# One list of threads at the end of attention, and three products of the last block on GpSimd instead of VectorE

## The chip, the cores and the metric

The kernel runs on one core of a Trainium2 chip. The metric is the device time of one execution in microseconds (us), a median over several executions. A profiled execution gives a trace beside it. Engines are called by the names of the profile: PE is TensorE, PEld its weight loads, DVE is VectorE, ACT is ScalarE, POOL is GpSimd, SP is SyncE, which issues most DMAs.

## What is computed

One layer of a transformer, in float32, on x of 4 x 1024 tokens with 256 channels. First a causal attention over the 1024 tokens with 16 heads of 16 and a linear bias by distance; then, with "tokens" and "batch" in other roles, a second attention in which each of the 1024 positions attends over the 4 rows of the batch, and a mixture of 8 experts in which each token takes the larger of its two best experts' numbers:

```
x = x + (softmax(q k^T / 4 + bias) v) @ w_proj.T        # q, k, v from layernorm(x)
u = layernorm(x)
q, k, v = split(u @ in_proj_w.T + in_proj_b)            # per token and row of the batch
attn = softmax(q[t] . k[s] / 4 over the 4 rows s)       # scores of 4 x 4 x 16 per position
h = layernorm(u + (attn v) @ out_w.T + out_b)
assign = max(top_2(softmax(h @ router_w.T + router_b)))
oe = gelu(h @ w1[assign].T + b1[assign]) @ w2[assign].T + b2[assign]
out = x + layernorm(h + oe)
```

## The kernel before

All of the time is in one function, fast_layer. (general_layer, behind a flag, is a fallback which isn't run with these inputs.) The order of the instructions on each engine is the order in which the program issues them; the program plans that order by a small model of costs while it is built.

**Attention** (up to about 606 us). The work goes by units of tokens and by rounds: score a round (matmuls into sk, exponential on ScalarE into p), mask with a select on GpSimd (line 1038), weigh it (matmuls of p with v into pv, line 1044), copy the result yt, and store it. Each round has slots into which the program places work for VectorE and TensorE that falls due (E_slot, D_slot, take_E, take_D, lines 2156 to 2326). A finished unit is divided by its sums of exponentials, projected by w_proj and added to x. For most units the sums go through DRAM (load_sums, invert, load_inverse, divide, project; lines 1104 to 1150): the product yc x su, then matmuls op<-wp,yc, then the addition (add_attended, line 1137). The last unit does it on the chip: a matmul adds up the slots (sum<-yt,slot_sum), VectorE takes the reciprocal and multiplies (yn; normalise, line 1172), four matmuls project (op<-wp_slots,yn; project_slots, line 1181), and the result is added to x.

**The fronts.** A front (line 1615) takes the 4 rows of the batch at 128 positions, a block, through the second attention up to the router. It is a generator that yields before each piece of work the letter of the engine that decides it and a cost. Its steps: statistics of the four x (norm_stats), their root on GpSimd (norm_root, line 828), u, transposes (ut), qkv by matmuls, four score products pr of 128 x 1024 each followed by a reduction (sc), the softmax, four weighted products pv of 128 x 1024 each followed by transposes into PSUM (ctp), copies (ct), matmuls with w_out (ao), additions to u, layer norm (rstd_h, by a root on GpSimd), the router, and the placing of tokens in lists by expert. There are 8 blocks, numbered 0 to 7. Fronts run between the rounds of attention; block 6 is under way at attention's end, and block 7, "the last block", follows it. In the last block the score and weighted products go one by one, with tile work between (lines 1703 to 1770).

**Expert tiles.** Each tile takes up to 128 tokens of one expert: GpSimd gathers their rows by an indirect DMA (given<-rows, line 1889), TensorE transposes (mtp), ScalarE scales (mt), TensorE multiplies by w1 (hid), ScalarE does the gelu (ge), TensorE multiplies by w2 (oe), VectorE takes statistics (stats_v), GpSimd or VectorE the root, VectorE makes the result in place in the gathered tile (given), and GpSimd clears a spare word (line 2005) and stores by an indirect DMA (out_dram<-given, line 2006). Groups of up to two tiles take their root on GpSimd (line 829); larger groups take it by a Newton step on VectorE (norm_root_v, line 833). 34 tiles are done: 18 from a first table, which needs the first six blocks alone, and 16 from a second table, which needs the last block's placing (the matmuls who, at 681 us). The gathered tiles live in N_GIVEN = 20 buffers, used in turn; LANDING = 2 keeps some of them free. The first four tiles have their experts' weights loaded by themselves; all later tiles use the whole of w1 and w2 in SBUF (load_layer, line 2395, three DMAs on SP for each).

**The end of attention and the tail.** Behind the last rounds (line 2376 on) the program issues one after another what is left of attention: what is due on VectorE, normalise(2) and normalise(3), project_slots, the last unit but one's division and projection, the last store of y and load of sums. Only then does it build `threads`, with block 7's front first, the unfinished fronts (block 6) and the preparation of the second table behind it, and plan them against the tiles: of the threads it takes the one that can begin first by the model, and a tile step where TensorE would be idle before it (lines 2440 to 2500). At least HELD_BACK = 5 tiles are kept for the time in which the second table is made.

Of the kernel before, what the change touches and what calls it, by code (L numbers as in the profile page):

```python
# [29 lines left out]
F32 = mybir.dt.float32  # L30
# [7 lines left out]
P = 128  # L38
# [26 lines left out]
TURNED = 2  # L65
EARLY = 0
N_OWN = 4
N_GIVEN, LANDING = 20, 2
N_W1 = 3
HELD_BACK = 5  # L70

TILE = (("PE", 2.6), ("DVE", 1.7), ("ACT", 1.9), ("POOL", 2.3))
TILE_HALF, LAG, COPIED, FIRST_BY, W1_THERE, LOAD_W2 = 1.3, 0.2, 1.0, 0.1, 14.0, 2.0
KQ_BUFS = 2
D_SLOT = 10.0
SWITCH, COLUMN, EXP_AT_ALL, EXP, READ = 0.2, 1 / 600, 0.17, 1 / 1200, 0.7
AHEAD, EARLY_BY, ROOT, OF_D = 1.0, 0.2, 1.4, 0.35
SUMS_BY, INVERTED_BY, Y_BY, DIVIDED_BY, PROJECTED_BY = 7.0, 14.0, 16.5, 26.0, 28.0
NEVER, HURRIED = 1e6, {SUMS_BY: 2.0, INVERTED_BY: 5.5, Y_BY: 7.5}
# [529 lines left out]
def fast_layer(ctx: ExitStack, tc: tile.TileContext, odd, x, wq, wk, wv, wp, w_in, w_out, w_r,  # L609
# [60 lines left out]
    def bank(name):  # L670
        if tail_banks:
            return tail_banks[0].tile([P, QC], F32, tag="m", name=name)
        if half_of:
            return half_of.pop()
        pair = pair_of_banks(name)
        halves[pair.tensor.name] = [], []
        half_of.append(pair[:, 1])
        return pair[:, 0]
# [51 lines left out]
    def wide(a):  # L730
        return a.unsqueeze(1).to_broadcast([P, B] + list(a.shape)[1:])
# [90 lines left out]
    def norm_stats(src, n, name, tag=""):  # L822
        tiles = norm_tiles(name, tag)
        for i in range(n):
            norm_one(tiles, i, src(i))
        return norm_end(tiles, n)
# [310 lines left out]
    def add_attended(u, pm):  # L1137
        n, i, size = units[u]
        at = xs[batches[n]][:, i:i + size].rearrange("p n c -> p (n c)")
        nc.vector.tensor_tensor(at, at, pm[:, :size * C], ALU.add)  # L1140

    def project(u):
        yc = held.pop(("y", u))
        pm = bank(f"op_{u}")
        for i in range(units[u][2]):
            for cc in range(CC):
                nc.tensor.matmul(
                    pm[:, i * C:(i + 1) * C], yc[:, cc, i * P:(i + 1) * P], wp_sb[:, cc],
                    start=cc == 0, stop=cc == CC - 1,
                )  # L1150
        add_attended(u, pm)


    slot_sum = const("slot_sum", [P, P])
# [14 lines left out]
                )  # L1169
            held["wp"].append(w)  # L1170

    def normalise(g):
        if g % 2 == 0:
            held["yn", g // 2] = ends.tile([P, 2, W], F32, tag="su", name=f"yn_{g}", bufs=2)
        yt, yn = (held[k, g // 2][:, g % 2, :P] for k in ("yt", "yn"))
        pm = bank(f"sum_{g}")[:, :P]
        nc.tensor.matmul(pm, slot_sum, yt, start=True, stop=True)
        nc.vector.reciprocal(yn, pm)
        nc.vector.tensor_tensor(yn, yn, yt, ALU.mult)

    def project_slots():
        pm = bank(f"op_{last_unit}")
        for g in range(G):
            nc.tensor.matmul(
                pm[:, :C], held["yn", g // 2][:, g % 2, :P], held["wp"][g // 2][:, g % 2],
                start=g == 0, stop=g == G - 1,
            )
        add_attended(last_unit, pm)


    def numbered(name, shape, pattern, up=0, base=0, dtype=F32, into=keep):
# [423 lines left out]
    def front(i, fact, more, last):  # L1615
# [1 line left out]
        xi = [xs[i // PC, t] for t in range(B)]  # L1617
        at_x = lambda t: xi[t][:, i % PC]
        rows_of = part.rows_of.rearrange("(k t p) c -> k p t c", t=B, p=P)[i]
        yield "E", 2.5  # L1620
        mv, rstd = norm_stats(at_x, B, f"u_{i}")
        yield "R", 1.2
        norm_root(rstd, B)
        yield ("A" if last else "P"), 1.9
# [71 lines left out]
            routed()  # L1696

        sc = fact.tile([P, B, B, H], F32, tag="sc", name=f"sc_{i}")
        for t in range(B):
            yield "E", 2.4, 0.9 if last else 0.0  # L1700
            if last:
                projected_qkv(t, QC, 3 * C + E)
            pr = fact.tile([P, B, C], F32, tag="pr", name=f"pr_{i}_{t}")
            nc.vector.tensor_tensor(pr, wide(qk[:, t, 0:C]), qk[:, :, C:], ALU.mult)
            nc.vector.tensor_reduce(
                sc[:, t], pr.rearrange("p s (h d) -> p s h d", d=D), AX.X, ALU.add
            )
# [16 lines left out]
        nc.vector.reciprocal(tot, tot)  # L1724
        nc.vector.tensor_tensor(sc, sc, each_s(tot), ALU.mult)

        def weighted(t):
            pr = fact.tile(
                [P, B, C], F32, tag="ctx" if last and t % 2 else "pr", name=f"pv_{i}_{t}"
            )  # L1730
            nc.vector.tensor_tensor(
                pr.rearrange("p s (h d) -> p s h d", d=D),
                vr[:, :, 0:C].rearrange("p s (h d) -> p s h d", d=D),
                sc[:, t].unsqueeze(3).to_broadcast([P, B, H, D]),
                ALU.mult,
            )
            return pr

        if last:

            ct = fact.tile(
                [P, CC, QC], F32, tag="turned", name=f"ct_{i}", bufs=TURNED if more else 2
            )

            def turned_sum(t, pr):
                pt = bank(f"ctp_{i}_{t}")[:, :C].rearrange("p (c q) -> p c q", q=P)

                for cc in range(CC):
                    for k in range(B):
                        nc.tensor.matmul(  # L1750
                            pt[:, cc], pr[:, k, cc * P:(cc + 1) * P], ident,
                            is_transpose=True, start=k == 0, stop=k == B - 1,
                        )
                nc.scalar.copy(ct[:, :, t * P:(t + 1) * P], pt)

            pr = None
            for t in range(B):
                yield "E", 1.3, 1.0 if t else 0.0
                if t:
                    turned_sum(t - 1, pr)  # L1760
                pr = weighted(t)
            yield "D", 1.0
            turned_sum(B - 1, pr)
            for t in range(B):
                for_later(t)
            store(("x", i), store_later)
        else:
            ctx_ = fact.tile([P, B, C], F32, tag="ctx", name=f"ctx_{i}")
            for t in range(B):
                yield "E", 2.3  # L1770
                pr = weighted(t)
                nc.vector.tensor_tensor(pr[:, 0:2], pr[:, 0:2], pr[:, 2:4], ALU.add)
                nc.vector.tensor_tensor(ctx_[:, t], pr[:, 0], pr[:, 1], ALU.add)
# [356 lines left out]
    def busy(on, cost, ready=0.0):  # L2130
        time[on] = max(time[on], ready) + cost
        return time[on]
# [119 lines left out]
    def projected(u):  # L2252
        n, i, size = units[u]
        c = batches[n][0]
        project(u)
        for k in range(PC * c + i, PC * c + i + size):
            n_projected[k] += 1
            if n_projected[k] == B and k < NT - 1:
                queue.append(front(k, fact, 1, False))
# [41 lines left out]
    def E_slot(k, some=True):  # L2301
        for cost, what in of_E.pop(k, []) + pop_due(due_E, time["PE"]):
            what()
            busy("DVE", cost)
        issue_stores(age=1)
        for it in stores:
            it[1] += 1
        load_next()
        if tables and fetching:
            experts.fetch()  # L2310
        take_E(some)
# [43 lines left out]
    for p in range(len(rounds) // 2):  # L2355
        then = p < len(rounds) // 2 - 1
        score_next(2 * p)
        E_slot(2 * p)
        D_slot(p, then)
        fill()  # L2360
        take_E(then)
        score_next(2 * p + 1)
        if len(waiting) > 2:
            weigh_next(waiting[:2])
            del waiting[:2]
        fill()
        E_slot(2 * p + 1, then)
# [6 lines left out]


    assert not of_E and not of_D, (sorted(of_E), sorted(of_D))

    take_E()
    for g in range(2, G):
        normalise(g)  # L2380
        busy("DVE", 1.3)
    project_slots()
    for _, what in pop_due(due_E, 2 * NEVER) + pop_due(due_D, 2 * NEVER):
        what()
    issue_stores(age=0)
    load_sums(last_unit)
    for it in running:
        it.ready = 0.0
    tail = ctx.enter_context(pool("tail", 1))
# [5 lines left out]
    def load_layer(sb, src):  # L2395
        for lo, hi in ((1, 3), (3, 5), (5, E)):
            nc.sync.dma_start(sb[:, lo - 1:hi - 1], src[:, lo:hi])
# [27 lines left out]
            n_bad, n_good, -1.0, float(B * NT * H), ALU.mult, ALU.add  # L2425
        )

    of_late = [(LOAD_W2, lambda: load_layer(w2_sb, w2))]

    late["at_place"] = ends.tile([P, 2 * B, P], BF16, tag="su", name="at_places", bufs=2)  # L2430

# [5 lines left out]

    threads = [Running(front(NT - 1, fact, 1, True))] + running + [Running(prepare_rest())]  # L2440
    free = {"PE": 0.0, "DVE": 0.0, "ACT": 0.0, "POOL": 0.0}
    threads[0].ready = 0.0
    engine_of = {"E": "DVE", "P": "DVE", "A": "ACT", "N": "ACT", "R": "POOL", "D": "PE", "d": "PE"}

    def begin(it):
        if it.kind == "DQ" and ("qkv",) in held or it.kind[1:] == "C" and part.placed < NT - 1:
            return 1e9
        return max(it.ready, free[engine_of[it.kind[0]]])

# [13 lines left out]
            threads.remove(it)  # L2463

    def tile_begin():
        return max(free["PE"], W1_THERE if experts.n_fetched > 2 * N_OWN else 0.0)

    def tile_step(finish=True):
        at = tile_begin()
# [135 lines left out]
```

## Time and profile before

| | us |
|---|---|
| median of 5 runs (lowest to highest) | 762.64 (762.23 to 764.65) |
| the profiled execution | 764.41 |
| its span in the trace | 762.7 |
| final weighing of attention begins | 603.67 |
| first score product of the last block | 634.40 |
| last matmul of its ao | 662.33 |
| TensorE's last matmul | 742.73 |
| last store of a tile ends | 751.83 |

| engine | busy us | share of the span |
|---|---|---|
| PE | 686.6 | 90% |
| PEld | 516.7 | 68% |
| DVE | 519.5 | 68% |
| ACT | 426.2 | 56% |
| POOL | 235.5 | 31% |

A line of the timeline has the start in us, the duration, engine, line, operation, output<-inputs with partitions x elements, and in brackets the idle time of the engine before it and what ended it. A group's line has its count, the busy time and the mean ns of one, and the idle time ahead with its releasers. Most instructions are recorded by one helper and stand at L590; they are told apart by the names of their tiles. A matmul of float32 is two rows in the trace. The table of windows gives each engine's busy time within a stretch, the granted TensorE clock as a share of full speed (PEclk), and the DMA engines' busy share.

### The profile page before, as it was taken

To read this page: it belongs to the slowest core of one execution; us is meant where nothing else is said; L and a number is where in the kernel's file an instruction comes from. 1 tells how busy PE (TensorE), PEld (TensorE's weight loads), DVE (VectorE), ACT (ScalarE), POOL (GpSimd) and SP (SyncE) were. 2 spreads that over 40 slices of the span, in tenths; PEclk is the share of its full clock that TensorE was granted. 3 is DMA by queue.
4 is the path that set the end of the run, shared out by engine and by line. 5 is a ranking of instruction groups with operands and counts; after the bars stand their busy time and mean duration, and the time that the engine had idled before them with its cause. 6 is when DMAs were issued, how large, how long until landed. Compare 5 with 4: busy or idle time off the path is not lost. (4 is left out here: it accounts for less than half of the span.)

```text
span 762.7 us, 21784 instructions
## 1 busy us (share of the span) xinstructions
PE 686.6 (90%) x8877; PEld 516.7 (68%) x8877; DVE 519.5 (68%) x1312; ACT 426.2 (56%) x647; POOL 235.5 (31%) x335
## 2 busy tenths in 40 slices
PE   3889899999999999999898999999999787989990
PEld 2667677675665766667567887678868655879980
DVE  4546437566996674889854163979769969699972
ACT  1446456563656574565556765658657435467750
POOL 4453213130332220023311130213212421268883
PEclk9999999999999999999899999999999989899995
DMA  7535453432363332323326543434343392154431
GB/s 217 154 114 174 153 181 118 136 118 82 91 190 99 102 107 93 109 88 104 121 77 211 179 150 93 165 113 146 113 137 102 89 310 96 33 169 145 147 103 35
DMA packets 70871, 98.46 MB, mean 129 GB/s; under 512 B 15408, under 2 KB 54635, under 8 KB 70252
## 3 DMA queue, kind: packets, MB, share of 16 engines
q1 hardware_dynamic: 58528, 67.82, 28.6%
q10 hardware_dynamic: 7884, 16.05, 6.6%
q0 software_dynamic: 4352, 13.11, 5.6%
q8 instruction: 73, 1.20, 0.6%
q14 instruction: 34, 0.28, 0.1%
HBM read 60.50 MB, written 34.59 MB: 125 GB/s over the span
## 5 line engine op out<-in xcount | busy, mean ns | idle before, releaser
L590 ACT ACTIVATE p<-sk 128x1024 f32<-128x1024 f32 (+1 forms) x320 | 288.0, 940 | 147.7 <-PE sk L590 120.8
L1038 POOL TENSOR_SCALAR_AFFINE_SELECT p<-p 128x512 f32<-128x512 f32 (+1 forms) x160 | 107.9, 679 | 403.1 <-ACT p L590 400.5
L590 PE MATMUL sk<-slots 32*128 32x128 f32 (+1 forms) x3456 | 178.1, 327 | 11.1 <-DVE kq L590 4.3
L590 PEld LDWEIGHTS sk<-slots 32*128 32x128 f32 x3456 | 135.0, 187 | 53.6 <-issue 24.2
L590 PE MATMUL pv<-p,v 128*32 128x128 f32 (+1 forms) x3456 | 145.3, 315 | 7.8 <-ACT p L590 4.0
L590 PEld LDWEIGHTS pv<-p,v 128*32 128x32 f32 x3456 | 96.0, 111 | 46.6 <-ACT p L590 8.0
L590 PE MATMUL qkvp<-w_in,ut 128*128 128x264 f32 (+1 forms) x240 | 83.5, 486 | 0.2 <-ACT ut L590 0.2
L590 PEld LDWEIGHTS qkvp<-w_in,ut 128*128 128x128 f32 x240 | 42.5, 190 | 28.8 <-issue 24.3
L590 PE MATMUL qkp<-xt,wqk 128*128 128x256 f32 x224 | 56.3, 396 | 0.2 <-ACT p L590 0.2
L590 DVE COPY kq<-qkp 128x512 f32<-128x512 f32 x28 | 19.1, 685 | 48.6 <-PE qkp L590 48.6
L590 PEld LDWEIGHTS qkp<-xt,wqk 128*128 128x128 f32 x224 | 41.4, 194 | 10.9 <-issue 3.3
L590 PE MATMUL hid<-mt,w 128*128 128x128 f32 x272 | 40.9, 287 | 2.6 <-ACT ge L590 1.7
L590 DVE TENSOR_TENSOR pv<-vr,sc 128x1024 f32<-128x1024 f32 x32 | 39.6, 1239 | 3.8 <-PE ctp L590 3.5
L590 ACT COPY qkv<-qkvp 128x512 f32<-128x512 f32 x28 | 16.4, 586 | 44.9 <-PE qkvp L590 44.7
L590 DVE COPY vr<-qkvp 128x264 f32<-128x264 f32 x28 | 12.1, 431 | 42.4 <-PE qkvp L590 42.4
L590 DVE TENSOR_REDUCE sc<-pr 128x64 f32<-128x1024 f32 x32 | 39.0, 1220 | 1.1
L590 DVE TENSOR_TENSOR pr<-qkv 128x1024 f32<-128x1024 f32 x32 | 39.2, 1224 | 0.5 <-ACT qkv L590 0.2
L1889 POOL DMA_INDIRECT given<-rows,rows x34 | 36.3, 1066 | 10.0 <-issue 7.9
L590 PEld LDWEIGHTS hid<-mt,w 128*128 128x128 f32 x272 | 36.6, 195 | 3.8 <-ACT ge L590 2.2
L2006 POOL DMA_INDIRECT out_dram<-given,out_rows x34 | 34.4, 1011 | 7.6 <-issue 3.6
L590 PE MATMUL oe<-w,ge 128*128 (+1 forms) x136 | 35.9, 387 | 0.0
L590 PE MATMUL vp<-wv,xt 128*128 128x256 f32 x128 | 34.4, 415 | 0.0
(327 smaller groups left out, 980.5 us busy)
## 6 DMA issues: line engine op xcount, KB each, us to landing
slots<-k SPq DMA_DIRECT2D x32, 320.0 KB
k<-kq SPq DMA_DIRECT2D x32, 256.0 KB
v<-v ACTq DMA_DIRECT2D x4, 1152.0 KB
x<-in_x_dram SPq DMA_DIRECT2D x16, 256.0 KB
y<-yt SPq DMA_DIRECT2D x16, 256.0 KB
rows<-x SPq DMA_DIRECT2D x32, 128.0 KB
slots<-k SPq DMA_DIRECT2D x16, 256.0 KB
rows<-u SPq DMA_DIRECT2D x8, 512.0 KB
```

Of the source, the lines that this page charges most:

```text
L590: ins = made(*args, **kwargs)
L1038: nc.gpsimd.affine_select(blocks, blocks, pattern=[[0, 2], [0, size], [1, P]], compare_op=ALU.is_ge, fill=0.0, base=0, channel_multiplier=-1,)
L1889: nc.gpsimd.indirect_dma_start(out=self.hx, out_offset=None, in_=t.rows_of, in_offset=bass.IndirectOffsetOnAxis(ap=t.rows_[:, self.j:self. ...
L2006: ins = nc.gpsimd.indirect_dma_start(out=out.rearrange("t n c -> (t n) c"), out_offset=bass.IndirectOffsetOnAxis(ap=t.table.out_rows[:, t. ...
```

## The change

1. **One list of threads.** What was issued in a row at attention's end becomes two threads, last_slots and last_but_one, ahead of block 7's front in `threads`. project and project_slots return their PSUM tile, and the caller adds it to x. normalise's matmul is split off (sum_slots). In the last pair of rounds E_slot doesn't issue VectorE's due work any more, so this too is planned with the threads. The front takes the statistics of x one by one; in the last block the third and fourth wait until both units have been added ("EX"). The weight loads of w1 and w2 go ahead of the last store of y and the sums on SP (LOAD_SUMS).
2. **Products on GpSimd in the last block.** Of the four score products pr, GpSimd makes the second and the fourth; of the four weighted products pv, the fourth. They share one buffer of 4 KB a partition ("shared", one deep).
3. **Room for it.** N_GIVEN goes from 20 to 18 and LANDING from 2 to 1.
4. The planner's costs: tiles begin at 9.5 (OWN_THERE) and 20 (W1_THERE, before 14) by the model's clock.

```
-N_GIVEN, LANDING = 20, 2
+N_GIVEN, LANDING = 18, 1
...
-        add_attended(u, pm)
+        return pm
...
-        yield "E", 2.5
-        mv, rstd = norm_stats(at_x, B, f"u_{i}")
+        tiles = norm_tiles(f"u_{i}")
+        yield "E", 1.2 if last else 2.5
+        for t in range(B):
+            if last and t == B - 2:
+                yield "EX", 1.4
+            norm_one(tiles, t, at_x(t))
+        mv, rstd = norm_end(tiles, B)
...
+        shared = lambda name: late["work"].tile([P, B, C], F32, tag="shared", name=name, bufs=1)
+        def multiplied(t, engine, pr):
+            engine.tensor_tensor(pr, wide(qk[:, t, 0:C]), qk[:, :, C:], ALU.mult)
+            return pr
         for t in range(B):
-            yield "E", 2.4, 0.9 if last else 0.0
+            if last and t % 2 == 0:
+                by_pool = multiplied(t + 1, nc.gpsimd, shared(f"pr_{i}_{t + 1}"))
+            yield "E", 1.2 if last and t % 2 else 2.4, 0.9 if last else 0.0
...
-            pr = None
-            for t in range(B):
+            pr, by_pool = None, weighted(B - 1, nc.gpsimd)
+            for t in range(B - 1):
                 yield "E", 1.3, 1.0 if t else 0.0
                 if t:
                     turned_sum(t - 1, pr)
                 pr = weighted(t)
-            yield "D", 1.0
-            turned_sum(B - 1, pr)
+            yield "D", 2.0
+            turned_sum(B - 2, pr)
+            turned_sum(B - 1, by_pool)
...
-        E_slot(2 * p)
+        E_slot(2 * p, then)
...
-    take_E()
-    for g in range(2, G):
-        normalise(g)
-        busy("DVE", 1.3)
-    project_slots()
-    for _, what in pop_due(due_E, 2 * NEVER) + pop_due(due_D, 2 * NEVER):
-        what()
-    issue_stores(age=0)
-    load_sums(last_unit)
...
-    of_late = [(LOAD_W2, lambda: load_layer(w2_sb, w2))]
+    of_late = [(LOAD_W2, lambda: load_layer(w2_sb, w2)), (LOAD_SUMS, lambda: load_sums(last_unit))]
...
+    def last_slots():
+        yield "D", 0.5
+        pms = [sum_slots(g) for g in range(2, G)]
+        yield "E", 2.6
+        for g in range(2, G):
+            normalise(g, pms[g - 2])
+        yield "D", 1.8
+        pm = project_slots()
+        yield "E", 0.5
+        add_attended(last_unit, pm)
+        added.append(last_unit)
+
+    def last_but_one():
+        u = last_unit - 1
+        yield "E", 0.5
+        divide(u)
+        yield "D", 0.9
+        pm = project(u)
+        yield "E", 0.5
+        add_attended(u, pm)
+        added.append(u)
```

In the compiled order of the instructions, these move on each engine:
- VectorE: yn_1 and the statistics of x_0 and x_1 stand right after the first weighted product of block 6; yc x su after its second; yn_2, yn_3 and the addition to x_2 after its third; then the fourth, the addition to x_3, ct's copy and the statistics of x_2 and x_3. The statistics and root of the first pair of tiles (stats_v_0) go from between the last block's first two weighted products to behind its router.
- TensorE: op<-wp,yc goes ahead of op<-wp_slots; one tile step (mtp of one tile, hid and oe of earlier ones) goes from ahead of the last block's transposes to behind its ao.
- GpSimd: pr_1 stands ahead of the fifth gather, pr_3 ahead of the sixth, pv_3 ahead of the eighth. In the tail two groups of two tiles fewer take their root on GpSimd.
- SP: the last store of y and the sums stand behind the loads of w1 and w2.

More of the change, by code (lines that the diff above doesn't have):

```diff
@@ L72 @@
 TILE = (("PE", 2.6), ("DVE", 1.7), ("ACT", 1.9), ("POOL", 2.3))
-TILE_HALF, LAG, COPIED, FIRST_BY, W1_THERE, LOAD_W2 = 1.3, 0.2, 1.0, 0.1, 14.0, 2.0
+TILE_HALF, LAG, COPIED, FIRST_BY, OWN_THERE, W1_THERE, LOAD_W2, LOAD_SUMS = (
+    1.3, 0.2, 1.0, 0.1, 9.5, 20.0, 8.0, 10.0,
+)
 KQ_BUFS = 2
@@ L76 @@
 SWITCH, COLUMN, EXP_AT_ALL, EXP, READ = 0.2, 1 / 600, 0.17, 1 / 1200, 0.7
+LAST_SUMS = 3.7
 AHEAD, EARLY_BY, ROOT, OF_D = 1.0, 0.2, 1.4, 0.35
@@ L1170, in load_slotted, with sum_slots, normalise @@
             held["wp"].append(w)
-    def normalise(g):
+    def sum_slots(g):
+        pm = bank(f"sum_{g}")[:, :P]
+        nc.tensor.matmul(pm, slot_sum, held["yt", g // 2][:, g % 2, :P], start=True, stop=True)
+        return pm
+    def normalise(g, pm=None):
         if g % 2 == 0:
@@ L1175, in normalise @@
         yt, yn = (held[k, g // 2][:, g % 2, :P] for k in ("yt", "yn"))
-        pm = bank(f"sum_{g}")[:, :P]
-        nc.tensor.matmul(pm, slot_sum, yt, start=True, stop=True)
+        if pm is None:
+            pm = sum_slots(g)
         nc.vector.reciprocal(yn, pm)
@@ L1187, in project_slots @@
             )
-        add_attended(last_unit, pm)
+        return pm
     def numbered(name, shape, pattern, up=0, base=0, dtype=F32, into=keep):
@@ L1698, in front @@
         sc = fact.tile([P, B, B, H], F32, tag="sc", name=f"sc_{i}")
+        shared = lambda name: late["work"].tile([P, B, C], F32, tag="shared", name=name, bufs=1)
+        def multiplied(t, engine, pr):
+            engine.tensor_tensor(pr, wide(qk[:, t, 0:C]), qk[:, :, C:], ALU.mult)
+            return pr
         for t in range(B):
-            yield "E", 2.4, 0.9 if last else 0.0
+            if last and t % 2 == 0:
+                by_pool = multiplied(t + 1, nc.gpsimd, shared(f"pr_{i}_{t + 1}"))
+            yield "E", 1.2 if last and t % 2 else 2.4, 0.9 if last else 0.0
             if last:
                 projected_qkv(t, QC, 3 * C + E)
-            pr = fact.tile([P, B, C], F32, tag="pr", name=f"pr_{i}_{t}")
-            nc.vector.tensor_tensor(pr, wide(qk[:, t, 0:C]), qk[:, :, C:], ALU.mult)
+            if last and t % 2:
+                pr = by_pool
+            else:
+                pr = multiplied(
+                    t, nc.vector, fact.tile([P, B, C], F32, tag="pr", name=f"pr_{i}_{t}")
+                )
             nc.vector.tensor_reduce(
@@ L1725, in front, with weighted @@
         nc.vector.tensor_tensor(sc, sc, each_s(tot), ALU.mult)
[L1727 to L1731, printed above, removed]
+        def weighted(t, engine=nc.vector):
+            if engine is nc.gpsimd:
+                pr = shared(f"pv_{i}_{t}")
+            else:
+                pr = fact.tile(
+                    [P, B, C], F32, tag="ctx" if last and t % 2 else "pr", name=f"pv_{i}_{t}"
+                )
+            engine.tensor_tensor(
                 pr.rearrange("p s (h d) -> p s h d", d=D),
@@ L2254, in projected @@
         c = batches[n][0]
-        project(u)
+        add_attended(u, project(u))
         for k in range(PC * c + i, PC * c + i + size):
@@ L2436, in prepare_rest @@
         part.prepare_rest(1)
-    threads = [Running(front(NT - 1, fact, 1, True))] + running + [Running(prepare_rest())]
-    free = {"PE": 0.0, "DVE": 0.0, "ACT": 0.0, "POOL": 0.0}
-    threads[0].ready = 0.0
+    added = []
+    def last_slots():
[18 more added lines that the diff above has]
+        added.append(u)
+    threads = (
+        [Running(last_slots()), Running(last_but_one()), Running(front(NT - 1, fact, 1, True))]
+        + running + [Running(prepare_rest())]
+    )
+    free = {"PE": LAST_SUMS, "DVE": 0.0, "ACT": LAST_SUMS + 0.5, "POOL": 0.0}
+    threads[0].ready = LAST_SUMS + 0.6
+    threads[1].ready = 3.0
     engine_of = {"E": "DVE", "P": "DVE", "A": "ACT", "N": "ACT", "R": "POOL", "D": "PE", "d": "PE"}
@@ L2446, in begin @@
         if it.kind == "DQ" and ("qkv",) in held or it.kind[1:] == "C" and part.placed < NT - 1:
+            return 1e9
+        if it.kind == "EX" and len(added) < 2:
             return 1e9
@@ L2465, in tile_begin @@
     def tile_begin():
-        return max(free["PE"], W1_THERE if experts.n_fetched > 2 * N_OWN else 0.0)
+        return max(free["PE"], W1_THERE if experts.n_fetched > 2 * N_OWN else OWN_THERE)
     def tile_step(finish=True):
```

## The prediction

> **What bounds the kernel now.** I read the page's busy shares first. TensorE is busy 90% of the span, which says little of a change that touches only the last 160 us, so I went on to the table of windows for those.
>
> ```profile
> core 0: us, PE busy (x) PEld busy (x) DVE busy (x) ACT busy (x) POOL busy (x), PEclk, DMA share, GB/s
> 600.00:610.00 10.00, 4.85 (x122) 3.86 (x112) 9.59 (x15) 1.83 (x4) 6.89 (x6) 1.00 0.45 124
> 640.00:650.00 10.00, 6.56 (x44) 5.59 (x43) 9.24 (x16) 6.09 (x12) 0.00 (x0) 0.88 0.01 2
> 690.00:700.00 10.00, 10.00 (x80) 9.26 (x79) 9.04 (x36) 7.33 (x17) 8.20 (x12) 1.00 0.44 143
> 740.00:750.00 10.00, 2.73 (x18) 2.09 (x16) 5.72 (x18) 0.38 (x1) 7.72 (x15) 0.83 0.24 77
> ```
>
> In the first two rows TensorE is half idle and VectorE is full: attention's end and the last block's scores wait for VectorE. GpSimd does nothing in the second row. From 690 TensorE is full; after 740 it is done and GpSimd still works. So next I took the tail's groups on GpSimd, 671.43 to 752 (last columns: busy time and mean ns of one; idle time before them and its releasers):
>
> ```profile
> L2006 POOL DMA_INDIRECT out_dram<-given,out_rows x34 | 34.4, 1011 | 7.6 <-issue 3.6 <-DVE given L590 2.7 <-DVE root_v L590 0.4
> L1889 POOL DMA_INDIRECT given<-rows,rows x23 | 24.2, 1053 | 6.8 <-issue 5.3 <-PE hid L590 0.6 <-DVE mv_v L590 0.3
> L829 POOL TENSOR_TENSOR rstd_v<-rstd_v,minus_half 128x2 f32<-128x2 f32 x5 | 3.7, 738 | 0.2
> ```
>
> A gather takes 1.05 and about 0.30 ahead of it, a store 1.01, its memset 0.12 and 0.19 between. 23 x 1.34 + 34 x 1.31 + 5 roots with their neighbours' gaps at 0.95 = 80.1 us, and from 671.43 to the last store's end at 751.83 are 80.4. GpSimd's queue, then, is never free behind 671: **GpSimd ends the tail**, 2.65 us per tile against TensorE's 2.48 (its tiles follow each other at that period). The end itself, GpSimd's and VectorE's rows of the timeline:
>
> ```profile
> 744.07 0.74 POOL L829 TENSOR_TENSOR rstd_v<-rstd_v,minus_half 128x2 f32<-128x2 f32 x1
> 744.85 0.48 DVE L590 SCALAR_TENSOR_TENSOR given<-given,rstd_v 128x256 f32<-128x256 f32 x1 [3.20 <-POOL rstd_v L829]
> ...
> 750.84 0.99 POOL L2006 DMA_INDIRECT out_dram<-given,out_rows  x1 [0.19 <-POOLq L2515]
> ```
>
> VectorE waits 3.20 us for a root that stands in GpSimd's queue behind stores. The chain of waits on the page starts at that last store, too. TensorE's last matmul is at 742.73; statistics, root, result and two stores need some 1.3 + 0.8 + 1.0 + 2.6 = 5.7 us behind it, so TensorE has about 3.4 us of slack.
>
> **The end of attention.** Rows of three engines:
>
> ```profile
> 600.45 2.02 POOL L1038 TENSOR_SCALAR_AFFINE_SELECT p<-p 128x256 f32<-128x256 f32 x2 [3.71 <-ACT p L590]
> 602.67 0.94 DVE L590 RECIPROCAL yn<-sum 128x128 f32<-128x128 f32 x1
> 603.67 1.69 PEld L590 LDWEIGHTS pv<-p,v 128*32 128x32 f32 x64 [2.61 <-DVE yn L590]
> 610.07 1.22 PE L590 MATMUL op<-wp_slots,yn 128*128 128x256 f32 x2 [2.48 <-DVE yn L590]
> ```
>
> The final weighing waits until VectorE has read a bank with yn_1 (603.61), though the selects are done at 602.47. In the new order yn_1 is ahead of VectorE's second product group, so the weighing starts near 602.6. Then I lay VectorE's new order end to end, at the old rows' lengths: yn_1 600.13 to 601.4; statistics of x_0 and x_1 (1.2) to 602.6; a product with its two folds (2.44, from 603.93 to 606.37) to 605.05; yc x su (0.42) to 605.5; the next product to 607.95; yn_2 and yn_3 (2.46) to 610.4; the addition to x_2; the last product to 613.05; the addition to x_3 to 613.5. The two projections, on TensorE until 615.4 in before, lie beside that. The block's transposes (2.6) end near 615.7 and not 618.1, so ct's copy is done at 616.4 and not 618.79: the ao matmuls, what follows on TensorE, and the last statistics (625.69, now 622.9) come **2.7 us** earlier. Statistics of x_2 and x_3 end at 617.2, the root 618.25, where it ended at 619.34; it covers the ao additions. So the last block's scores start at 631.7 and not 634.40. If yn_1's wait alone went, it would be 1.05.
>
> On SP, y's last store and the sums now follow the loads of w1 and w2, which wait for them in before and start at 610.79. Nobody reads the sums before the eighth tile after the table, and TensorE needs w1 and w2 only from the fifth tile on: I cost this at nothing; the DMA share of 0.96 in 620 to 630 moves ten us forward, beside VectorE's work. Without the cover a gather would land late, some 1 us.
>
> **The scores.** In before four pairs on VectorE, 10.0 us:
>
> ```profile
> 634.40 1.22 DVE L590 TENSOR_TENSOR pr<-qkv 128x1024 f32<-128x1024 f32 x1 [0.20 <-ACT qkv L590]
> 635.66 1.22 DVE L590 TENSOR_REDUCE sc<-pr 128x64 f32<-128x1024 f32 x1
> ...
> 644.45 0.58 DVE L590 TENSOR_REDUCE top<-sc 128x64 f32<-128x256 f32 x1
> 645.07 0.42 DVE L590 TENSOR_TENSOR sc<-sc,top 128x256 f32<-128x256 f32 x1
> ```
>
> Now GpSimd makes products 1 and 3. No row shows a GpSimd product of this size. Below, its selects: 0.43 for 256 elements, 0.64 for 512, so 0.84 ns an element and 0.21 fixed, 1.07 for 1024 read once, 1.93 read twice. Above, a root's 0.9 (2 to 4 elements wide, hence start-up) and two readings, 2.6. I take 2.2, between the two that read both inputs. And they collide: the select pair above took 2.02 instead of 0.85 while VectorE made a two-input product (600.13 to 601.36, then folds); alone at 356.15 one took 1.71, which is VectorE's 1.21 and 0.5. At 163.42 and 589.83 selects beside a reduction kept 0.43 and 0.64. So I let the GpSimd product lie beside reductions, and not beside products. pr_0 1.22; pr_1 2.2, beside the reduction of 0; the reduction of 1, 1.22; pr_2 1.22; pr_3 2.2, since its one buffer is free only after reduction 1 and it then collides with pr_2; the last reduction 1.22; four hand-overs at 0.06. That is 4.88 + 2 x 2.2 + 0.24 = **9.5, a gain of 0.5**. Ends: 7.6 at 1.07 (gain 2.4) and 10.3 at 2.6 (loss 0.3). With no collision at all pr_3 starts under pr_2 and the gain is about 2.5. VectorE's wait for pr_1 and pr_3 has nothing urgent behind it but the scores themselves; behind them on GpSimd wait gathers 4 to 6, used by tiles that TensorE reaches only after ao, some 20 us later.
>
> The Trainium skill prices this too: "GPSIMD Engine Reference", section 3.1, has 4497 ns measured for an addition of 2048 elements, and half of it is 2.25 us, an estimate; the sum by it is 9.6. Its page "SBUF — State Buffer" ("Who interferes with whom") speaks against the change: a VectorE instruction with two SBUF inputs and a GpSimd one that reads SBUF contend for one shared interface, and a reduction never does. The selects above agree, at 1.71 against 0.43; by that rule the gain stays 0.5, and without it it would be 2.5.
>
> **The weighted products.**
>
> ```profile
> 650.07 1.22 DVE L590 TENSOR_TENSOR pv<-vr,sc 128x1024 f32<-128x1024 f32 x1
> 654.74 2.36 DVE L590 TENSOR_TENSOR pv<-vr,sc 128x1024 f32<-128x1024 f32 x2 [3.46 <-PE ctp L590]
> ```
>
> The third and fourth wait 3.46 us for TensorE's transposes, so VectorE isn't the limit: moving the fourth gains 0 to 0.2, and stats_v_0, which stood between the first two (1.4 us), leaves the way. GpSimd's product needs only to be ready some 8 us after the softmax; it collides with three of VectorE's (3 x 1.22 + 2.2 = 5.9), still in time. I take 0.2. TensorE idles in before from 644.51 for ScalarE (2.18) and 1.26 more, around the exponential's table load. The same is there after, but one tile step (2.48) that TensorE did ahead of the transposes now lies behind ao: the idle time is longer by it and TensorE owes it to the tail.
>
> **The sum.** ao ends at 662.33 in before; now 2.7 + 0.5 + 0.2 = 3.4 us earlier. Behind it the order is much the same; VectorE runs stats_v_0 there (+0.2), and a gap around the counts is some 0.5 shorter. Then:
> - GpSimd's queue: 751.83 - 3.4 + 0.2 - 1.9 = 746.7, the 1.9 for two roots fewer (2 x 0.95), whose groups take a Newton step on VectorE; VectorE has 0.7 to 1 us free in each 10.
> - TensorE: 742.73 - 3.4 + 2.5 - 0.5 = 741.3, and 5.7 behind it: 747.0.
>
> The two are level, so they will wait for each other now and then: I add 0.7, 747.7 instead of 751.83, **4.1 us less**. The profiled execution took 764.41 (span 762.7): 760.3 by that. It lies 1.8 above the median of the five runs, 762.64, so I forecast 758.6 for the median, and say 758.8. The buffers, 18 instead of 20, cost nothing: the gather for the second table's first tile needs the first store, which stands ten places ahead in the queue.
>
> **Rivals.** About 0.2% (1.5 us) is what a measurement of this kernel can tell from no change.
> 1. *No collision.* A GpSimd product reads beside VectorE's. For it: selects beside reductions. Against: 600.45. Gain 4.1 + 2.0 = 6.1: 756.5. Chance 0.12.
> 2. *Attention's end gives nothing* beyond a little, as the new VectorE order is as full as the old (9.59 of 10 busy at 600) and the addition to x_2 waits for a projection at a half clock (0.66 in 610 to 620). 4.1 - 2.7 = 1.4, or less with another 0.5 lost to the tile step left over: 761.2 to 761.7, within 0.2%. Or the products keep GpSimd at 2.6 and the gains thin out. Chance 0.16.
> 3. *Slower: GpSimd's products are the bound.* Place: the scores. Each us above 2.2 costs 2, as VectorE waits for both pr_1 and pr_3. At 450.94 GpSimd was kept out for 2.1 us by back-to-back VectorE products, and here it starts next to them. 4.1 is used up at 2.2 + 2.05 = 4.25 us; from there it's slower, and at 5.5 us the loss is 2.5: 765.1. Against it: all bounds end at 2.6. The tile step left over would add to it. Chance 0.18, the base for things that the rows don't show.
> 4. *The change doesn't do what it says*: the planner leaves the order as it was. In the compiled order of instructions every step named here has moved; left out.
>
> Forecast 0.54. The range reaches from rival 1 at its better end, 756.0, to a slower case short of rival 3's price, 763.6; about 2 in 10 lie outside. Faster by over 0.2%: 0.54 + 0.12 + 0.03 of rival 2 = 0.69; same 0.14; slower 0.17.
>
> **What would show it.** Scores in 9.5 us, GpSimd's product near 2.2 beside a reduction and longer beside VectorE's; the final weighing at 602.6; the first score product at 631.7; ao's end near 659; five roots in the tail become three; the last store at 747.5. Wrong: a GpSimd product over 4 us, a score phase over 10, TensorE ending after 743, or a second half-clock stretch in the tail.

## The result, and the profile after

The change made the kernel slower: a median of 766.9 us (29 runs, 761.4 to 768.03) against 762.88 (57 runs of before, 759.67 to 768.22), a ratio of 1.0042 with a 95% interval of 1.0032 to 1.0053. The forecast was 758.8, in 756.0 to 763.6. The profiled execution took 766.39 us, its span is 764.2. Almost every step that was forecast is there in the trace, and nearly as large as forecast. The loss arises behind the last of them.

The table of windows of after, in the columns of the one shown of before:

```profile
core 0: us, PE busy (x) PEld busy (x) DVE busy (x) ACT busy (x) POOL busy (x), PEclk, DMA share, GB/s
600.00:610.00 10.00, 5.41 (x59) 3.70 (x47) 9.69 (x17) 0.27 (x1) 5.94 (x5) 1.00 0.75 243
640.00:650.00 10.00, 7.80 (x46) 6.76 (x47) 8.13 (x10) 4.26 (x10) 4.71 (x2) 0.71 0.20 60
670.00:680.00 10.00, 6.22 (x73) 5.33 (x71) 9.10 (x37) 5.34 (x11) 4.87 (x7) 1.00 0.53 155
680.00:690.00 10.00, 10.00 (x63) 9.02 (x64) 9.22 (x33) 5.01 (x12) 7.15 (x10) 0.83 0.34 103
```

The row to look at is 670 to 680: TensorE is busy for 6.22 us where it had 9.95 in before (8.84 from 680 to 690, where before has its who), while VectorE is as full as ever. The next row has a granted clock of 0.83; before had the full clock from 654.5 to 746. TensorE's and GpSimd's rows of the timeline say what they wait for:

```profile
676.52 0.22 PE L593 MATMUL hid<-chosen,b_bf 128*128 128x128 bf16 x1
679.96 0.66 PE L593 MATMUL oe<-ident,mt 128*128 128x128 f32 x2 [3.22 <-DVE given L593]
```
```profile
679.79 1.03 POOL L2036 DMA_INDIRECT out_dram<-given,out_rows  x1 [3.92 <-DVE given L593]
```

Both wait for VectorE's `given`. The products oe go in pairs to three PSUM banks, so the ninth tile's oe needs the bank of tiles 2 and 3, and that is read last by their results given. VectorE's own rows in that time:

```profile
668.82 0.19 DVE L593 TENSOR_TENSOR rank<-place,hot 128x32 f32<-128x32 f32 x1 [3.64 <-PE place L593]
...
672.55 0.82 DVE L593 TENSOR_TENSOR in_tile<-numbers,found 128x640 bf16<-128x640 f32 x1
...
676.08 0.21 DVE L593 COPY who_f<-who 128x60 f32<-128x60 f32 x1
...
678.43 0.48 DVE L593 SCALAR_TENSOR_TENSOR given<-oe,mv_v,rows 128x256 f32<-128x256 f32 x1
```

It idles 3.64 us before rank, then makes the second table (in_tile to at_w, 678.5), and only then gets to given. In before the same four instructions stand ahead of the table, and fill just the time in which VectorE waits for the placing:

```profile
672.38 0.48 DVE L590 SCALAR_TENSOR_TENSOR given<-oe,mv_v,rows 128x256 f32<-128x256 f32 x1
672.96 0.48 DVE L590 SCALAR_TENSOR_TENSOR given<-given,rstd_v 128x256 f32<-128x256 f32 x1
...
675.56 0.18 DVE L590 TENSOR_TENSOR rank<-place,hot 128x32 f32<-128x32 f32 x1
```

The order changed because results are issued by tile steps, as part of the work of later tiles. The shorter products leave the plan one tile step fewer ahead of the transposes; with it, the whole series of finishing steps moved back by one, and the results of tiles 2 and 3 fell behind the second table.

To compare two executions, I count from one event that both orders have unchanged, the end of a short idle time of TensorE (0.64 us) at 578.10 in before and 576.05 in after. (The 2.05 us between these belong to neither order: the instructions ahead are the same.)

| us from that event | before | after | change |
|---|---|---|---|
| first score product | 56.31 | 53.13 | -3.18 |
| scores end (top begins) | 66.36 | 62.46 | -3.90 |
| last ao ends | 84.23 | 78.73 | -5.50 |
| last who ends | 104.15 | 99.38 | -4.77 |
| TensorE's last matmul ends | 164.63 | 167.43 | +2.80 |
| last store ends | 173.74 | 177.78 | +4.04 |

The last row agrees with the change of the median (+4.0). From who to TensorE's end after needs 68.05 us, and before 60.48: 7.57 more. They are the tile step that now lies behind (2.48), the wait (3.22), and 680.0 to 683.4 at half clock (3.4 us that count for half, 1.7): 7.4.

### The profile page after: what moved, and what is told of

Read it like the earlier page. It is cut to its first block, busy times and chain, and to the rows that moved or that the text cites. A ratio compares the mean times of both kernels' runs of the same rounds, so it can differ in the third digit from the quotient of the medians.

```text
span 764.2 us, 21792 instructions
## 1 busy us (share of the span) xinstructions
PE 685.3 (90%) x8877; PEld 516.3 (68%) x8877; DVE 518.1 (68%) x1319; ACT 426.2 (56%) x647; POOL 242.7 (32%) x336
## 5 line engine op out<-in xcount | busy, mean ns | idle before, releaser
L1041 POOL TENSOR_SCALAR_AFFINE_SELECT p<-p 128x512 f32<-128x512 f32 (+1 forms) x160 | 105.8, 665 | 403.5 <-ACT p L593 400.8
L593 PEld LDWEIGHTS qkvp<-w_in,ut 128*128 128x128 f32 x240 | 42.5, 190 | 28.8 <-issue 24.5
L593 PEld LDWEIGHTS qkp<-xt,wqk 128*128 128x128 f32 x224 | 41.0, 192 | 10.5 <-issue 3.3
L1919 POOL DMA_INDIRECT given<-rows,rows x34 | 38.3, 1125 | 10.0 <-issue 7.4
L2036 POOL DMA_INDIRECT out_dram<-given,out_rows x34 | 34.4, 1012 | 15.7 <-DVE given L593 10.8
L593 ACT ACTIVATE mt<-mtp,columns 128x128 f32<-128x128 f32 x68 | 27.4, 453 | 19.3 <-PE mtp L593 19.2
L593 DVE TENSOR_TENSOR pr<-qkv 128x1024 f32<-128x1024 f32 x30 | 36.7, 1224 | 0.6 <-ACT qkv L593 0.4
```

Source lines behind the costliest of these rows:

```text
L593: ins = made(*args, **kwargs)
L1041: nc.gpsimd.affine_select(blocks, blocks, pattern=[[0, 2], [0, size], [1, P]], compare_op=ALU.is_ge, fill=0.0, base=0, channel_multiplier=-1,)
L1919: nc.gpsimd.indirect_dma_start(out=self.hx, out_offset=None, in_=t.rows_of, in_offset=bass.IndirectOffsetOnAxis(ap=t.rows_[:, self.j:self. ...
L2036: ins = nc.gpsimd.indirect_dma_start(out=out.rearrange("t n c -> (t n) c"), out_offset=bass.IndirectOffsetOnAxis(ap=t.table.out_rows[:, t. ...
```

## The experiments

Theory A is the reading above: the wait of TensorE behind the table, which comes with the planner's new place for tile steps. Theory B blames the new threads themselves, C the GpSimd products themselves, D the fewer buffers, E the new groups of the tail. The ratios below are to before on the same chip, measured beside the run; a difference in us is the ratio's unless medians are named. The runs were on three chips on which before takes 790.35 (numbers 1 to 4), 791.7 (5 to 8) and 795.15 us (9 to 12), some 28 to 32 more than on the first. Most of that is in the tail: in number 6, the run nearest to before, 24.5 us of it lie between who and TensorE's end. There ScalarE stands still for 3 to 9 us at a time with nothing in the profile that releases it but "remote". So ratios are compared, and of the traces, mainly the parts ahead of the tail. The change has 1.0042, 1.0031 and 1.0032 on three chips, so its ratio carries over from chip to chip; on the chip of numbers 1 to 4 it wasn't run, and the comparisons of these with it rest on that.

**1. The threads alone.** The change, with the old lines for pr and pv:

```
-            if last and t % 2 == 0:
-                by_pool = multiplied(t + 1, nc.gpsimd, shared(f"pr_{i}_{t + 1}"))
-            yield "E", 1.2 if last and t % 2 else 2.4, 0.9 if last else 0.0
+            yield "E", 2.4, 0.9 if last else 0.0
...
-            pr, by_pool = None, weighted(B - 1, nc.gpsimd)
-            for t in range(B - 1):
+            pr = None
+            for t in range(B):
```

> The new list of threads, 18 buffers and the new order of the loads; all products of the last block on VectorE as in before. The tile steps then stand as in before (11 tiles begun ahead of the matmuls who, given of tiles 2 and 3 ahead of the second table on VectorE). Theory A (the loss is the wait of TensorE for given behind the table, which comes with the products' shorter plan): no such wait here, and 2 to 3.5 us faster than before. Theory B (the threads themselves lose, by the last block's late statistics or the loads moved on SP): 2 to 5 us slower than before. Theory C (GpSimd's products take VectorE's port and lose): like A here.

Measured: 785.93 against 790.35, ratio 0.9921 (0.9893 to 0.9949): 6 us faster, more than A's 2 to 3.5, and TensorE has no wait for given. B falls.

**2. The products alone.** Before with the change's lines for pr and pv, and 18 buffers:

```
-N_GIVEN, LANDING = 20, 2
+N_GIVEN, LANDING = 18, 1
...
+            if last and t % 2 == 0:
+                by_pool = multiplied(t + 1, nc.gpsimd, shared(f"pr_{i}_{t + 1}"))
...
+            pr, by_pool = None, weighted(B - 1, nc.gpsimd)
```

> Before with the three products on GpSimd, and 18 buffers. The plan then has one tile step fewer ahead of who (10), and given of tiles 2 and 3 behind the table. Theory A: the scores 0.5 to 0.8 us shorter, but TensorE waits some 3 us for given behind the table and has one step (2.5 us) more behind it, so 4 to 8 us slower than before, and slower than the whole change by the 2.7 us of the threads. Theory B: 0 to 1 us faster than before. Theory C: 1 to 4 us slower, without a wait of TensorE behind who.

Measured: 803.04, ratio 1.0133 (1.0104 to 1.0161), 10.5 us slower (12.7 by the medians), more than A's 4 to 8. The trace has TensorE's wait for given (2.61), and the scores in 9.34 us. It has a stop of 4.90 ahead of who, too, of the kind that these chips have. So the half of the change that loses is the one with the products; whether by the order that it brings or by itself is for numbers 3, 4 and 11.

**3. The results ahead of the placing.**

```
         if kind == "DQ":
             held["qkv",] = True
+        if kind == "DC":
+            experts.finish()
```

> The whole change, and given of tiles 2 and 3 issued ahead of the last block's placing, in VectorE's idle time, instead of behind the second table; still one tile step fewer ahead of who. Theory A: TensorE's 3.2 us behind who go, and a stretch of half clock behind them (3.4 us at half speed, 1.7 us): 3 to 5 us faster than the whole change, within 1 us of before. Theory B and C: no more than 0.5 us from the whole change.

Measured: 788.0, ratio 0.9956 (0.9928 to 0.9984); the change itself is at 1.0042 in the result and at 1.0031 in number 5. That is some 0.8%, 6 us, under the change, where A said 3 to 5, and 3.5 us under before, where it said within 1. VectorE's given lies ahead of rank, in the time that was idle, and TensorE no longer waits for it:

```profile
666.12 0.48 DVE L593 SCALAR_TENSOR_TENSOR given<-oe,mv_v,rows 128x256 f32<-128x256 f32 x1
666.70 0.48 DVE L593 SCALAR_TENSOR_TENSOR given<-given,rstd_v 128x256 f32<-128x256 f32 x1
...
670.90 0.18 DVE L593 TENSOR_TENSOR rank<-place,hot 128x32 f32<-128x32 f32 x1
```

TensorE isn't without waits behind who in this trace: 1.77 us for mt and 4.26 for ge, with ScalarE stopped ahead of both. finish() also closes the groups of the tail as before had them (GpSimd takes 7 roots rstd_v in this trace, as in before, and 5 in after), so two things moved; numbers 9 and 10 are to part them.

**4. The tile step back in its place.** One planned cost, 1 us higher:

```
-        yield "P", 1.6
+        yield "P", 1.6 + (1.0 if last else 0.0)
```

> The whole change, with one cost of the planner 1 us higher (the last block's division by the softmax's total), so that the tile step stands ahead of the last block's transposes again, as in before, and given ahead of the table. Theory A: both losses go: 3 to 5 us faster than before, about 759. Theory B: 1 to 3 us slower than before. Theory C: like the whole change, 3 us slower than before.

Measured: 786.44, ratio 0.9955 (0.993 to 0.9981). That is 3.5 us under before, as A said. The GpSimd products are all there, and one planned cost takes the whole loss away; B's and C's numbers for this run are wrong by over 0.5%. It isn't faster than the threads alone, though.

**5. The change again**, with no edit.

> The change itself, once more, beside the variants: what it stands at against before on the chip that this call falls on. All theories: 3 to 5 us slower than before if this chip is as the first. Theory A: TensorE waits about 3.2 us behind who for given, in this trace too.

Measured: 795.9 against 791.7, ratio 1.0031 (0.9999 to 1.0063). The wait is there, 2.61 us.

**6. The buffers alone.** In before:

```
-N_GIVEN, LANDING = 20, 2
+N_GIVEN, LANDING = 18, 1
```

> Before with 18 gathered buffers and one kept free, instead of 20 and two; nothing else. Theory A: within 1 us of before, since the gathers' order is the same. Theory D (the loss is in the fewer buffers: gathers wait for stores): 2 to 4 us slower than before.

Measured: 789.78, ratio 0.9978 (0.9953 to 1.0003): no loss. D falls.

**7. The threads with 20 buffers.** Number 1, and

```
-N_GIVEN, LANDING = 18, 1
+N_GIVEN, LANDING = 20, 2
```

> The new threads with 20 buffers and two kept free, the products on VectorE: the change without its GpSimd part and without what that costs in room. Theory A: 2.5 to 4 us faster than before. Theory D: 2 us better than with 18 buffers, which were at 0.992 of before on the chip of the first four runs.

Measured: 786.79, ratio 0.9938 (0.9919 to 0.9957), as with 18 buffers (0.9921). D falls here too.

**8. The step back, and only the scores on GpSimd.** Number 4, and

```
-            pr, by_pool = None, weighted(B - 1, nc.gpsimd)
-            for t in range(B - 1):
+            pr = None
+            for t in range(B):
```

> The whole change with the tile step put back (the planner's cost 1 us higher) and only the two score products on GpSimd; all weighted products on VectorE. Theory A: like the whole change with the step put back, 3 to 5 us faster than before; the weighted product decides nothing, as it waits for TensorE either way (0 to 0.3 us).

Measured: 787.62, ratio 0.9939 (0.9912 to 0.9965): as number 4 within their intervals. The weighted product makes no difference that these two show.

**9. Only the results moved.** At the same place as in number 3, but the groups stay as the change has them:

```
+        if kind == "DC":
+            for stages in list(experts.finishing):
+                if next(stages, experts) is experts:
+                    experts.finishing.remove(stages)
```

> The whole change, and only the results given of tiles 2 and 3 go from behind the second table to ahead of the last block's placing on VectorE; the groups of the tail and their 7 roots on GpSimd stay as the change has them. Theory A: the wait behind who (3.2 us) and the half clock behind it (1.7 us) go: 4 to 5 us faster than the change, about 0.998 of before or a little under. Theory E (it is the new groups of the tail that cost, and moving given alone does little): within 1.5 us of the change.

Measured: 797.09, ratio 1.0007 (0.9975 to 1.0038), beside the change at 800.82, 1.0032 (0.9988 to 1.0076), on the same chip. The ratios are 2.0 us apart (the medians 3.7), less than the 4 to 5 expected, and the intervals overlap: the time shows neither A's gain nor that there is none. The trace shows that the wait is gone, oe follows hid at once:

```profile
689.96 0.22 PE L593 MATMUL hid<-chosen,b_bf 128*128 128x128 bf16 x1
690.02 0.39 PE L593 MATMUL oe<-ident,mt 128*128 128x128 f32 x2
```

**10. Only the groups as before.**

```
-                if len(group) > 2 or not late["wide"] or self.waiting() < 6:
+                if len(group) > 2 or not late["wide"] or self.waiting() < 6 or late["n_out"] < 4:
```

> The whole change, given as late as there, but tiles 4 and 5 close a group of two behind the table as in before, so that the tail has the groups and the 9 roots on GpSimd of before. Theory A: the wait stays: within 1.5 us of the change. Theory E: 3 us or more faster than the change.

Measured: 799.55, ratio 1.0062 (1.0031 to 1.0093), 2.4 us over the change (1.3 under it by the medians) and not told apart from it. The wait stays:

```profile
684.41 0.44 PE L593 MATMUL oe<-ident,mt 128*128 128x128 f32 x2 [2.61 <-DVE given L593]
```

The groups alone take nothing off; E falls in that form. Whether they help once given is early, as in number 3, isn't shown.

**11. The products alone, with the results ahead of the placing.** Number 2, and

```
+        if kind == "DC":
+            experts.finish()
```

> Before with the three products on GpSimd and 18 buffers, and given of tiles 2 and 3 ahead of the last block's placing. Without that it was at 1.013 of before. Theory A: the products as such gain or cost little: 0.997 to 1.002 of before, and at least 6 us faster than with the late given. Theory C (the products cost by themselves): still 1.006 or more.

Measured: 794.01, ratio 0.9997 (0.996 to 1.0033), against 1.0133 for number 2. The results of two tiles moved, with the groups of the tail that follow from it, are worth 1.4% here, some 11 us. That is far more than the wait (2.61 us in number 2, with no half clock behind it) explains; the two runs are of different chips, and the rest stays open. C falls: the products by themselves cost nothing that this measurement can tell. Nor do they gain.

**12. The change as the yardstick of 9 to 11**, with no edit.

> The change itself beside these three, as their yardstick on this chip: 1.003 to 1.006 of before by all theories.

Measured: 800.82, ratio 1.0032 (0.9988 to 1.0076).

## Where the prediction was right, and where it was wrong

**The end of attention: right.** The scores were to begin 2.7 us earlier; they began 3.18 earlier by the table. With the threads alone they began 53.29 and 51.93 us behind the same event (numbers 1 and 7), against 59.53 and 59.29 in before's order on the same two chips (numbers 2 and 6). The final weighing doesn't wait for yn_1 any more; in after its matmuls run without a gap:

```profile
597.78 3.24 PE L593 MATMUL pv<-p,v 128*32 128x128 f32 x112
```

This half of the change is all of its worth that the runs show: 0.6 to 0.8%.

**The scores: right.** 9.5 us were forecast, 9.33 measured, and 9.31 to 9.34 in the other runs with GpSimd's products. A product was to take 2.2 us and to collide with VectorE's:

```profile
629.18 1.23 DVE L593 TENSOR_TENSOR pr<-qkv 128x1024 f32<-128x1024 f32 x1 [0.36 <-ACT qkv L593]
630.44 1.22 DVE L593 TENSOR_REDUCE sc<-pr 128x64 f32<-128x1024 f32 x1
632.66 1.22 DVE L593 TENSOR_REDUCE sc<-pr 128x64 f32<-128x1024 f32 x1 [1.00 <-POOL pr L1716]
```
```profile
629.29 3.33 POOL L1716 TENSOR_TENSOR pr<-qkv 128x1024 f32<-128x1024 f32 x1 [7.73 <-ACT qkv L593]
...
633.97 3.25 POOL L1716 TENSOR_TENSOR pr<-qkv 128x1024 f32<-128x1024 f32 x1
```

GpSimd's 3.33 are the 1.1 until VectorE's product ends (630.41) and 2.2 for its own. The reduction beside it keeps its 1.22. That is what the Trainium skill's page "SBUF — State Buffer" ("Who interferes with whom") says of the shared interface. Of the two gains in the prediction, 0.5 with that collision and 2.5 without it, the measured 0.72 (10.05 to 9.33) fits the first. One of the prediction's comparisons was uneven: its 1.71 us was a select of 512 elements, and beside a reduction such a one took 0.64; 0.43 is the time for 256.

The weighted product was to wait for three of VectorE's; it waited for one, and VectorE's second waited for it (last section).

**But the scores' gain goes no further.** From the scores' end to the first transpose before has 8.46 us, after 7.94 with a tile step fewer, and with the step put back 10.38 (number 4). The reason is in ScalarE's order: the exponential now stands ahead of an earlier tile's mt, and TensorE, which runs out of tile work sooner, waits for that 3.93 us, where it waited 2.18. Before, then after:

```profile
646.69 0.44 PE L590 MATMUL mtp<-ident,given 128*128 128x128 f32 x2 [2.18 <-ACT mt L590]
```
```profile
640.75 0.69 PE L593 MATMUL mtp<-ident,given 128*128 128x128 f32 x2 [3.93 <-ACT mt L593]
```

From the first score product to ao's end, numbers 4 and 8 take 28.03 and 28.33 us, and the threads alone 27.84 and 27.60: no less. I had taken the 0.5 as time won; it was time in which TensorE had tile work, and it was given back at once.

**The first step that failed is the sum behind ao.** It had TensorE's end as "742.73 - 3.4 + 2.5 - 0.5", which priced the moved tile step as 2.5 us of TensorE's and as nothing else. A tile step carries VectorE's and GpSimd's part of older tiles with it. What is missing is TensorE's wait for their results, 3.22 us, and the half clock that follows, 1.7. TensorE was to end at 741.3; it ended at 743.48 (counted from the common event, 2.80 later than in before), and both that ("after 743") and a half-clock stretch in the tail stand among the prediction's own signs of being wrong. The list of moves on VectorE in the section on the change names stats_v_0, and leaves out that given of tiles 2 and 3 went past the table; I had read the order for what moved ahead of ao, not behind it.

**The second is "GpSimd ends the tail".** Its queue was full in before from 671 on, and I concluded that TensorE has 3.4 us of slack and that two roots fewer give 1.9. In after, GpSimd's groups from 671.43 on have idle times with real releasers:

```profile
L2036 POOL DMA_INDIRECT out_dram<-given,out_rows x32 | 32.4, 1012 | 15.4 <-DVE given L593 10.8 <-issue 3.2 <-DVE root_v L593 0.4
L832 POOL TENSOR_TENSOR rstd_v<-rstd_v,minus_half 128x2 f32<-128x2 f32 x3 | 2.2, 733 | 2.9 <-DVE rstd_v L593 2.9
```

10.8 us of idle time for given, and still the last store ends 10.35 us behind TensorE's last matmul, where before had 9.11. In the experiments, whose tails have long stops, it's 5.3 to 11.3. So a queue that is full for 80 us isn't needed for such an end. By the rows of after it comes from the order of the last groups; no run changed that order alone:

```profile
735.14 0.98 POOL L2036 DMA_INDIRECT out_dram<-given,out_rows  x1 [3.27 <-DVE given L593]
738.98 0.71 POOL L832 TENSOR_TENSOR rstd_v<-rstd_v,minus_half 128x2 f32<-128x2 f32 x1 [2.87 <-DVE rstd_v L593]
...
745.10 0.98 POOL L2036 DMA_INDIRECT out_dram<-given,out_rows  x1 [0.19 <-issue]
746.10 0.74 POOL L832 TENSOR_TENSOR rstd_v<-rstd_v,minus_half 128x2 f32<-128x2 f32 x1
```

GpSimd idles 3.27 us for the first result of a group of four. The root at 738.98 stands between the stores of that group, so the other three wait behind it for another 2.87; then five stores stand ahead of the next root. I had put 5.7 us behind TensorE's end, the least that could be, and taken the other 3.4 for slack.

Added up: forecast -3.9 at who, +2.5 in TensorE's tail, -2.7 behind it, -4.1 in all; measured -4.77, +7.57, +1.24, +4.04. The last ao ended 5.50 us earlier and not 3.4: the prediction let TensorE idle for all 2.48 of the moved step, and its two waits there grew by only 1.5 (3.93 and 1.01 against 2.18 and 1.26).

**The rivals.** None of them was it. Rival 3 had the right sign by the wrong mechanism: the GpSimd product took 2.2 behind VectorE's and not over 4.25. Rival 4 was put aside because the order showed that all steps had moved. That view should have been asked the other question: what else moved.

**What is shown, and what stays open.** That the loss comes with the tile step's new place is shown: put back, it takes the loss away (number 4), and so do early results together with before's groups (3 and 11). What the wait alone is worth isn't: on the first chip it is read from one trace, with the half clock 4.9 of the 7.57 us; early results alone gave 2.0 us that the intervals don't tell from nothing (9), and 3 and 11 gave more than the wait explains. On the chips of the experiments the wait is 2.61 us, without a half clock behind it (2, 5, 10 and 12), and something else goes with the step's place there: in all seven traces in which the step lies behind ao (2, 3, 5 and 9 to 12) ScalarE stops for 4.3 to 7.2 us within 9 us of who, and in none of the five with the step in its place (1, 4, 6, 7 and 8) does it stop so within 20 us. The experiments don't part the two. A version that beats both kernels is the threads alone, numbers 1 and 7.

## What to carry to other kernels

When a planner builds the order, a shorter cost for one step moves others past each other: compare the two orders to their very end on every engine, and for each instruction that moved behind a long series, name the buffer that it frees and who needs that next. A queue that is full for a long time isn't yet what sets the end; take the last instructions and ask of each what released it. And time won on an engine ahead of a hand-over counts only if the engine that takes over isn't behind in that place.

## What the runs showed of the hardware

- Two VectorE products beside GpSimd's weighted product took 4.09 us, where two take 2.4 to 2.5: the first kept 1.22, the second took 2.95, until GpSimd was done at 644.71 and 1.08 more. VectorE is held up as GpSimd is. The other runs with this product beside two of VectorE's have the same 2.95 and 2.87:

```profile
641.70 4.09 DVE L593 TENSOR_TENSOR pv<-vr,sc 128x1024 f32<-128x1024 f32 x2
```
```profile
641.84 2.87 POOL L1760 TENSOR_TENSOR pv<-vr,sc 128x1024 f32<-128x1024 f32 x1 [2.12 <-DVE sc L593]
```

- A wait of TensorE wasn't always followed by a half clock: behind 3.22 us in after it was (680.0 to 683.4), behind 2.61 us in numbers 2, 5, 10 and 12 it wasn't. In these four a half-clock stretch of 6.8 us, around the stop ahead of who, had ended 1.7 to 2.6 us before the wait began.
- On the chips of the experiments ScalarE stops in the tail, in number 4 for 6.0 and 4.3 us, and TensorE behind it. Neither the trace of before nor that of after has such a stop:

```profile
ACT ge L593 <- remote: 9.3, 3, 4.3
PE hid L593 <- ACT ge L593: 7.4, 3, 4.0
```

These are the waits of number 4 from 660 on (us in all, times, longest). What holds ScalarE there isn't settled.
